# Rows of a second modulation: loaded two ahead of the low-rank factors, multiplied in the convolution's program order

## The chip, the cores and the metric

The kernel runs on one core of one Trainium2 chip. The metric is the time of one launch on the device, in microseconds (us). The engines are PE (TensorE, the matrix engine), DVE (VectorE), ACT (ScalarE), POOL (GpSimd) and SP (SyncE, which here only issues DMAs). Every engine works through its own instructions in order, and an instruction that waits holds back all that stand behind it on that engine.

## The reference

```python
x = L0_attn_u                                       # (4, 1024, 2048)
mod = (silu(L0_c) @ L0_wmod).reshape(4, 6, 1, -1)   # wmod: (2048, 6 * 2048)
sa, ca, ga, sb, cb, gb = (mod[:, i] for i in range(6))
ga, gb = ((2 * (g >= 0) - 1) * max(abs(g), 0.25) for g in (ga, gb))
h = layernorm(x) * (1 + ca) + sa
x = x + ga * (causal_conv(h, K) + D * h)            # K: S4 kernel of length 2048, along the last axis
h = layernorm(x) * (1 + cb) + sb
x = x + gb * (h @ W.T + bias + sum_e w[e] * (h @ A[e].T) @ Bf[e].T)   # w = coeffs * scales
```

So there are two modulated layers: a long convolution along the 2048 features, and a 2048 x 2048 linear layer with 16 low-rank updates. The first layer needs sections 0, 1 and 2 of `mod`, the second needs sections 3, 4 and 5.

## The kernel before

The 4096 rows of x are taken as 32 tiles r of 128 rows.

**Modulation.** Section by section (1, then 0 and 2, later 4, 3 and 5), `wmod` is read as 16 rows of 128 x 2048 float32 (1 MB each) per section. `mod_load` (L320) issues such a row on SP's DMA queue, and `mod_mm` (L325) multiplies it: four matmuls of 32 output rows, side by side in the array, which add into one PSUM tile `modps`. The rows of the second modulation take turns in the `WM = 3` buffers of the pool `wmp`, so a fourth load waits on SP until the first product has been made.

**Convolution.** For each tile r: load (`conv_load`, L563), statistics (L548 to L72), normalisation (L558), then `conv_prep`: PE transposes in four quarters (L579), ACT applies scale and shift (L583) and casts to float16 (L593), DVE makes the remainders (L594) and the sums (L591). `conv_mm` then multiplies (L616) with Toeplitz blocks of K in three families, into PSUM tiles `ya` and `yb`; ACT copies the first family out as `qs` (L629), DVE finishes y (L633 to L643). `conv_post` stores y to DRAM (L658) and lets ACT take its squares (L662). x of tile r+2 is loaded while tile r is multiplied. Tiles 0 and 1 are multiplied early, with the first modulation's products between them, and are finished late (L652, L653).

**Low-rank merge.** `prep_lora` loads A (`la`, 2 MB, SP queue, L434) and squares it on ACT (L440), then loads B (`lb`, 2 MB, ACT's own queue, L449), scales it on ACT (L453), squares it (L457), scales again (L467) and casts (L468). `merge` (eight times) adds the product of the factors (PE `lps`, L494) to a block of W (loaded by L486) and writes seven Strassen blocks to DRAM.

**Linear layer.** From about 930 us on, a Strassen multiplication (L752) reads these blocks.

**Order.** A scheduler builds the order of each engine: it takes instructions by their place in the program (their priority) and by when its own cost estimates say that they can start. `tc.issue_after(i)` keeps what is inside it behind instruction `i` in that order; it adds no wait of its own on the chip. Inside tile r, `PLAN` tells at ten ticks what is to be issued beside the multiplication. "S" calls `step()`, which on every second call from tile 3 on advances `rest()`: two steps of the merge, then one row of `section(sec, (wmp,))` (load and product together), and so on:

```python
if r > EARLY and calls[0] % 2 == 0:
    with tc.issue_after(k.lasta.ins), tc.issue_after(k.lastv.ins):
        next(fill)
```

Here `lasta` and `lastv` are the last copy of `qs` and the last L633 of the convolution so far.

Of the kernel before, what the change touches and what calls it, by code (L numbers as in the profile page):

```python
# [34 lines left out]
class Net:  # L35
# [561 lines left out]
    def conv_mm(self, pl, hs, x, tick, early, pace, y=None):  # L597
        nc, v = self.nc, self.nc.vector
        hc, hs = hs
        if y is None:  # L600
            y = pl["y"].tile([P, D], F32, tag="y", name="y")
        yv = y.rearrange("p (j e t) -> p j e t", e=2, t=P)
        if not early:
            gv = self.gat.rearrange("p (j e t) -> p j e t", e=2, t=P)
        sums = pl["sm"].tile([P, 2], F32, tag="sums", name="sums")

        def family(ps, f, q, first):
            pf = ps.rearrange("p j t -> p (j t)")
            last = 4 * q + 3
            for i in range(last + 1):  # L610
                o = P * max(0, i - 4 * q)
                k0 = P * max(0, 4 * q - i)
                with pace(3 * (512 - o)):
                    for x, z in ((0, 0), (0, 1), (1, 0)):
                        h = hs[x][:, i] if f == 0 else hc[x][:, 2 * i + 2 - f]
                        nc.tensor.matmul(  # L616
                            pf[:, o:512], h, self.kf[f][z][:, ds(k0, 512 - o)],
                            start=first, stop=(i == last and (x, z) == (1, 0)), skip_group_check=True,
                        )
                        first = False  # L620
                if i == 3 and q == 1:
                    tick()

        for q in range(2):
            jj = slice(4 * q, 4 * q + 4)
            pa = self.cps.tile([P, 4, P], F32, tag="pa", name="ya")
            family(pa, 0, q, True)
            qs = pl["t"].tile([P, 4, P], F32, tag="qs", name="qs")
            self.lasta = nc.scalar.copy(qs, pa)  # L629
            tick()  # L630
            pb = self.cps.tile([P, 4, P], F32, tag="pb", name="yb")
            family(pb, 2, q, True)
            self.lastv = v.tensor_tensor(yv[:, jj, 1, :], pb, qs, ADD)  # L633
            if not early:
                v.tensor_tensor(yv[:, jj, 1, :], yv[:, jj, 1, :], gv[:, jj, 1, :], MUL)
            tick()
            family(pa, 1, q, False)
            sl = ds(1024 * q, 1024)
            if early:
                nc.scalar.copy(yv[:, jj, 0, :], pa)  # L640
            else:
                v.tensor_tensor(yv[:, jj, 0, :], pa, gv[:, jj, 0, :], MUL)  # L642
                v.scalar_tensor_tensor(y[:, sl], y[:, sl], 1.0, x[:, sl], MUL, ADD, accum_out=sums[:, q : q + 1])  # L643
            tick()
        return y, sums
# [182 lines left out]
WM, WMS = 3, 3  # L828
# [17 lines left out]
def net(ctx: ExitStack, tc: tile.TileContext, io):  # L846
    nc = tc.nc
    k = Net(ctx, tc, io)
# [6 lines left out]
    def pool(stack, name, bufs, side="left"):  # L855
        return stack.enter_context(tc.tile_pool(name=name, bufs=bufs, side=side, reuse_waits="tile"))
# [6 lines left out]
    wmp = pool(right, "wm", WM, "right")  # L863
# [2 lines left out]
    k.kpool = pool(left, "kt", 1)  # L866
    k.prep_mod(msm)

    def section(sec, pools):
        for q in range(16):  # L870
            if q == 0:
                k.mod_begin()
            k.mod_mm(k.mod_load(pools[q % len(pools)], sec, q), q)
            yield
        if sec == 0:
            k.sa = k.mod_column(msm, k.kpool, "sa", 0.0)
            k.hinv = k.fold_scale(msm, k.ca, k.sa, "fs1")
        elif sec == 1:
            k.ca = k.mod_column(msm, k.kpool, "ca", 1.0)
        elif sec == 2:  # L880
            k.gas, (k.gad,) = k.mod_gate(msm, "gad")
        elif sec == 4:
            k.cb = k.mod_column(msm, k.cst, "cb", 1.0)
        elif sec == 3:
            k.sb = k.mod_column(msm, k.cst, "sb", 0.0)
        else:
            _, k.gbd = k.mod_gate(msm, "gbd", io["bias"])
        yield

    def merges():  # L890
        yield from k.prep_lora(pl["lora"], pl["mrg"])
        for c in range(HC):
            yield from k.merge(pl["lora"], pl["mrg"], c)
# [3 lines left out]
    def take(g, n):  # L897
        for _ in range(n):
            next(g, None)
# [13 lines left out]
    def prep(r, shift=True):  # L913
        return k.conv_prep(pl, r, xs[r], sts.pop(r), hs, shift)
# [15 lines left out]
    for _ in section(1, (wms, wmp)):  # L930
        if n in KT:
            with tc.issue_after(k.last.ins), tc.high_priority():
                take(toe, 1)
        if n == X0:
            load(0)
        n += 1
    with tc.high_priority():
        stats(0)
        k.early_scale(msm)
    load(1)  # L940
    rows = (x for sec in (0, 2) for x in section(sec, (wms, wmp)))
    p = prep(0, False)
    take(p, 1)
# [49 lines left out]
    y2 = stp.tile([P, D], F32, tag="kb", name="y2")  # L993

    def rest():
        mods = (x for sec in (4, 3, 5) for x in section(sec, (wmp,)))
        n = 0
        for _ in mer:
            yield
            n += 1  # L1000
            if n % MR == 0:
                next(mods, None)
                yield
        for _ in mods:
            yield
        k.ginv = k.fold_scale(msm, k.cb, k.sb, "fs2", k.winv)
        yield

    fill = rest()
    p2l = ExitStack()  # L1010
    pr, wc, lf = {}, {}, {}
# [44 lines left out]
    stats(3)  # L1056
    nxt = prep(3)
    take(nxt, 1)
    cols[0] = 0

    def behind(n):
# [143 lines left out]
```

## Time and profile before

| | |
|---|---|
| median of 3 runs | 2148.39 us (2144.52, 2148.39, 2148.89) |
| profiled execution | 2145.24 us, of which the span from first to last instruction is 2143.4 us |
| mean granted TensorE clock | 0.989 |
| busy, share of the span | PE 2075.1 us (97%), DVE 1307.7 us (61%), ACT 925.1 us (43%) |
| HBM | 329 MB read, 155 MB written, 226 GB/s over the span |
| products of all 96 modulation rows (L325) | 116.2 us of PE, 26.8 us of idle time before them |

A timeline row gives start and length in us, the engine, the line, the operation, output and inputs, how many instructions are merged in it, and in brackets how long the engine was idle before it and what ended that. A row of the windows view gives a stretch, its length, the busy time and count of PE, PE's weight loads, DVE, ACT and POOL, the granted clock (1.00 is full), the share of DMA time and GB/s.

### The profile page before, as it was taken

Reading aid. Unit: us, or ns where it says so; the run is one execution under the profiler, and the core shown is the slowest. Engines: PE = TensorE matmul, PEld = TensorE weight load, DVE = VectorE, ACT = ScalarE, POOL = GpSimd, SP = SyncE. Lnnn points to the kernel's source line nnn. Section 1 sums busy time; section 2 is a strip of 40 time slices with the busy share of each in tenths; the row PEclk is TensorE's granted clock in tenths of the full one; section 3 lists DMA queues with packets and bytes.
Section 4 is the critical chain, followed back from the end, with each engine's and each line's share of the span. In section 5 each row is a group of like instructions: output and inputs, shape, how many; then the busy total and the mean of one; then the engine's idle time right before and its main releaser. Section 6 shows DMA issues by size and latency. Waiting matters only on the chain.

```text
span 2143.4 us, 28478 instructions
## 1 busy us (share of the span) xinstructions
PE 2075.1 (97%) x11121; PEld 1021.8 (48%) x11121; DVE 1307.7 (61%) x2358; ACT 925.1 (43%) x1703; POOL 7.0 (0%) x19
## 2 busy tenths in 40 slices
PE   6998799999999999999999999999999999999999
PEld 1344354555445555644545545545444444444444
DVE  5529699998889999756565565565432323232323
ACT  1425786677756877655554454455200000000000
POOL 0000000000000000000000000000000000000000
PEclk8999999999999999999999999999999999999999
DMA  9995846786776554387465565564795545555542
GB/s 400 417 371 197 314 163 250 285 309 240 281 274 247 187 191 174 124 336 281 172 246 191 184 241 184 197 241 180 270 350 165 188 150 171 168 165 166 177 153 74
DMA packets 127812, 486.21 MB, mean 227 GB/s; under 512 B 13672, under 2 KB 14088, under 8 KB 96446
## 3 DMA queue, kind: packets, MB, share of 16 engines
q1 hardware_dynamic: 126624, 479.65, 61.4%
q10 hardware_dynamic: 526, 2.63, 0.3%
q8 instruction: 87, 1.43, 0.3%
q0 software_dynamic: 528, 2.11, 0.2%
q14 instruction: 47, 0.39, 0.0%
HBM read 329.04 MB, written 155.30 MB: 226 GB/s over the span
## 4 chain that ended last, share of the span: by engine, by line
PE 64%; DVE 13%; ACT 5%; DMA 4%; issue 2%; ACTq 0%; SPq 0%; DVEq 0%
PE fZ L752 22%; PE fX L752 15%; PE fY L752 15%; PE ya L616 4%; PE tp L702 3%; DVE wch L522 2%; PE lps L494 2%; PE yb L616 2%; ACT t L583 1%; DVE st L548 1%; DVE hc L594 1%; DVE y L643 1%; DMA x<-in_x 1%; DMA we<-in_WT 1%; DVE hs L594 1%
## 5 line engine op out<-in xcount | busy, mean ns | idle before, releaser
L752 PEld LDWEIGHTS <-lf 128*128 128x128 f16 x5400 | 528.4, 98 | 621.1 <-issue 3.3
L752 PE MATMUL fZ<-w,lf 128*128 128x512 f16 (+1 forms) x2328 | 513.8, 377 | 1.3 <-ACT p L760 0.8
L752 PE MATMUL fX<-w,lf 128*128 128x512 f16 x1536 | 342.8, 379 | 1.4 <-DVE y L642 1.4
L752 PE MATMUL fY<-w,lf 128*128 128x512 f16 x1536 | 342.0, 379 | 0.0
L616 PEld LDWEIGHTS <-hc 128*128 128x128 f16 x2304 | 214.0, 98 | 213.8 <-issue 51.3
L770 DVE TENSOR_TENSOR xo<-xo,gb 128x512 f32<-128x512 f32 x128 | 87.7, 690 | 237.7 <-DMA xo<-x1d 224.4
L583 ACT ACTIVATE t<-tp,sa,ca 128x128 f32<-128x128 f32 x480 | 189.3, 476 | 38.2 <-PE tp L579 31.7
L616 PE MATMUL ya<-kh,hs 128*128 128x512 f16 (+3 forms) x768 | 194.6, 327 | 6.0 <-ACT hs L593 4.1
L616 PE MATMUL ya<-kh,hc 128*128 128x512 f16 (+3 forms) x768 | 192.4, 328 | 7.0 <-ACT qs L629 6.7
L616 PE MATMUL yb<-kh,hc 128*128 128x512 f16 (+3 forms) x768 | 194.0, 328 | 0.3 <-DVE hc L594 0.3
L760 ACT COPY p<-fZ 128x512 f32<-128x512 f32 x64 | 37.2, 582 | 286.0 <-PE fZ L752 272.1
L616 PEld LDWEIGHTS <-hs 128*128 128x128 f16 x1152 | 106.8, 98 | 106.4 <-issue 20.6
L760 ACT COPY p<-fX 128x512 f32<-128x512 f32 x32 | 18.8, 586 | 317.2 <-PE fX L752 242.1
L704 ACT ACTIVATE gt<-tp,sb,cb 128x256 f32<-128x256 f32 x256 | 125.0, 576 | 62.0 <-PE tp L702 60.5
L325 PE MATMUL modps<-wm,sct 128*32 128x512 f32 x768 | 116.2, 646 | 26.8 <-DMA wm<-in_wmod 19.5
L616 PE MATMUL ya<-kl,hc 128*128 128x512 f16 (+3 forms) x384 | 125.8, 328 | 0.0
L616 PE MATMUL yb<-kl,hc 128*128 128x512 f16 (+3 forms) x384 | 125.5, 327 | 0.0
L616 PE MATMUL ya<-kl,hs 128*128 128x512 f16 (+3 forms) x384 | 125.2, 326 | 0.0
L775 DVE TENSOR_TENSOR fin<-fX,gb 128x512 f32<-128x512 f32 x32 | 22.1, 692 | 127.4 <-PE fX L752 127.3
L594 DVE TENSOR_TENSOR hc<-t,hc 128x512 f16<-128x512 f32 x128 | 87.5, 684 | 8.2 <-ACT hc L593 7.9
L494 PE MATMUL lps<-lbh,lac 128*128 128x512 f16 x256 | 84.7, 379 | 5.4 <-DVE we L496 3.9
L715 DVE TENSOR_TENSOR lf<-gt,lf 128x1024 f16<-128x1024 f32 x64 | 76.7, 1219 | 18.1 <-ACT lf L714 18.1
(274 smaller groups left out, 2224.7 us busy)
## 6 DMA issues: line engine op xcount, KB each, us to landing
wm<-in_wmod SPq DMA_DIRECT2D x96, 1024.0 KB
lfd<-lf SPq DMA_DIRECT2D x112, 512.0 KB
lf<-lfd SPq DMA_DIRECT2D x112, 512.0 KB
x<-in_x SPq DMA_DIRECT2D x32, 1024.0 KB
x1d<-y SPq DMA_DIRECT2D x32, 1024.0 KB
x<-x1d SPq DMA_DIRECT2D x32, 1024.0 KB
xo<-x1d SPq DMA_DIRECT2D x128, 256.0 KB
out<-xo SPq DMA_DIRECT2D x127, 256.0 KB
```

The costliest lines, as they stand in the source:

```text
L325: self.last = self.nc.tensor.matmul(self.modps[32 * g : 32 * g + 32, :], self.sct[:, j].rearrange("p r b -> p (r b)"), w[:, ds(512 * g, 512)],
L494: nc.tensor.matmul(ps, la[:, x, k, h], y[:, k, osl], start=(n == 0), stop=(n == 5))
L522: v.tensor_tensor(hl[:, :, 1, :], tv, hl[:, :, 0, :], SUB)
L583: nc.scalar.activation(t[:, k], tp[:, k], AF.Identity, bias=self.sa[:, c, b : b + 1], scale=self.ca[:, c, b : b + 1],)
L594: v.tensor_tensor(lo[:, sl], src, hi[:, sl], SUB)
L616: nc.tensor.matmul(pf[:, o:512], h, self.kf[f][z][:, ds(k0, 512 - o)], start=first, stop=(i == last and (x, z) == (1, 0)), skip_group_chec ...
L702: nc.tensor.transpose(tp[:, c, r], xs[r][:, ds(P * (c0 + c), P)], self.ident)
L704: nc.scalar.activation(t[:, c0 + c], tp[:, c], AF.Identity, bias=self.sb[:, c0 + c, b : b + 1], scale=self.cb[:, c0 + c, b : b + 1],)
L715: v.tensor_tensor(hl[:, :, 1, :], s, hl[:, :, 0, :], SUB)
L752: nc.tensor.matmul(ps[name][:, cols], lf[i][:, k, x, :], wc[i][k // 4][:, k % 4, y, cols], start=(first and n == 0), stop=(n == 3 * HC - 1 ...
L760: nc.scalar.copy(t, ps[name])
L770: v.tensor_tensor(x, x, self.gbias[:, h], ADD)
```

## The change

The rows of sections 4, 3 and 5 are taken from one list, `order`. `fetch()` issues the load of the next row of that list and puts it into `ahead`. Ahead of the loop over tiles, two rows are fetched, behind the last load issued before (`k.lastw`). Each step of a section then makes the product of the oldest fetched row, kept behind the last matmul of the convolution that has been written so far (`lastc`), and fetches one more row. Sections 1, 0 and 2 work as before. `self.lastc` is new in `conv_mm`.

```diff
-                        nc.tensor.matmul(
+                        self.lastc = nc.tensor.matmul(
...
-    def section(sec, pools):
+    def section(sec, pools=None):
         for q in range(16):
             if q == 0:
                 k.mod_begin()
-            k.mod_mm(k.mod_load(pools[q % len(pools)], sec, q), q)
+            if pools:
+                k.mod_mm(k.mod_load(pools[q % len(pools)], sec, q), q)
+            else:
+                with tc.issue_after(k.lastc.ins):
+                    k.mod_mm(ahead.pop(0), q)
+                fetch()
             yield
...
+    order, ahead = [(sec, q) for sec in (4, 3, 5) for q in range(16)], []
+
+    def fetch():
+        if order:
+            ahead.append(k.mod_load(wmp, *order.pop(0)))
...
-        mods = (x for sec in (4, 3, 5) for x in section(sec, (wmp,)))
+        mods = (x for sec in (4, 3, 5) for x in section(sec))
...
     stats(3)
     nxt = prep(3)
     take(nxt, 1)
+    with tc.issue_after(k.lastw.ins):
+        for _ in range(WM - 1):
+            fetch()
```

## Prediction

> **What bounds the kernel now.** I read the busy times first: PE is busy for 2075.1 of 2143.4 us, so only 68 us can be won by removing waits, and PE work that leaves an idle stretch for a full one is paid in full. Then the windows view, cut where the changed products lie:
>
> ```profile
> 150.00:222.80 72.80, 62.32 (x373) 31.60 (x370) 59.57 (x132) 36.07 (x79) 0.56 (x1) 0.98 0.68 249
> 222.80:248.20 25.40, 15.10 (x92) 4.20 (x91) 8.50 (x23) 15.29 (x31) 0.00 (x0) 0.87 0.88 360
> 248.20:345.00 96.80, 93.18 (x549) 51.27 (x549) 90.26 (x188) 74.32 (x149) 0.61 (x1) 1.00 0.58 219
> 345.00:930.00 585.00, 570.02 (x3531) 309.04 (x3530) 520.54 (x1084) 413.97 (x850) 0.41 (x1) 1.00 0.63 233
> ```
>
> PE has 10.3 us free in 222.8 to 248.2, but only 3.6 in the 96.8 us after. What fills and what ends the holes is in PE's timeline:
>
> ```profile
> 178.79 2.78 PE L325 MATMUL modps<-wm,sct 128*32 128x512 f32 x24
> 185.65 0.28 PE L616 MATMUL ya<-kh,hs 128*128 128x256 f16 x1 [4.08 <-ACT hs L593]
> ...
> 222.79 3.11 PE L325 MATMUL modps<-wm,sct 128*32 128x512 f32 x22
> 225.83 0.66 PE L579 MATMUL tp<-ident,n 128*128 128x128 f32 x4
> 233.55 1.91 PE L325 MATMUL modps<-wm,sct 128*32 128x512 f32 x2 [7.07 <-DMA wm<-in_wmod]
> 239.34 0.39 PE L616 MATMUL ya<-kh,hs 128*128 128x512 f16 x1
> 248.21 0.38 PE L616 MATMUL ya<-kh,hc 128*128 128x512 f16 x1 [0.66 <-ACT qs L629]
> ```
>
> The 7.07 us look like the cost of a late weight row. But ACT's and DVE's timelines of the same stretch show another chain:
>
> ```profile
> 221.07 0.41 ACTq L449 DMA_DIRECT2D lb<-in_BfT  x1
> 233.41 3.89 ACT L453 ACTIVATE lb<-lb,lwt 128x2048 f32<-128x2048 f32 x2 [9.86 <-DMA lb<-in_BfT]
> 238.25 0.39 ACT L593 CAST hs<-sm 128x256 f16<-128x256 f32 x1
> 247.57 0.59 ACT L629 COPY qs<-ya 128x512 f32<-128x512 f32 x1
> ```
> ```profile
> 238.66 0.42 DVE L594 TENSOR_TENSOR hs<-sm,hs 128x256 f16<-128x256 f32 x1 [11.76 <-ACT hs L593]
> ```
>
> ACT waits for the low-rank factor B; the casts of tile 5 stand behind that wait; DVE waits 11.76 us for them; PE's `ya` at 239.34 needs their result. From 233.41 to 248 ACT is without a gap of half a microsecond, and its `qs` releases PE at 248.21. I call 248.21 the mark. So the products sit in a hole that ACT makes.
>
> **Which products move.** In the order of instructions before, 12 of the 48 rows of the second modulation are multiplied ahead of the mark, 36 behind it. In the changed order two are ahead of it and 46 behind; the last product keeps its place, near the end of the convolution. Ten rows move from the hole into the full stretch. Nothing else is added to PE.
>
> **Cost of a moved row.** At 349.84 a convolution matmul starts (this kind repeats every 0.215 us), the product starts at 350.15, and the next convolution matmul at 351.15. Without the product it would start at 350.06, so a row costs 1.09 us. Ten rows: +10.9 us, say +11.0.
>
> **What the old place saves.** Ahead of the mark nothing, unless ACT gets there sooner. The three products at 178.79 lie before a wait for ACT that ends at 185.65 either way (PE then idles 6.9 instead of 4.1 us). Those at 185.97 (1.92 us, a single matmul that stood apart) and 202.28 (1.07 us) shorten PE's way to 212.00, but there it waits 1.19 us for DVE, which is itself held until 210.46 by the small loads of `lws`, issued at the same place as before. One product still stands there. From 222.79 on PE would idle longer: saved 0.
>
> A longer hole may cool PE: at 186 to 188 the windows show a clock of 0.50 after the 4.08 us idle, at 188 to 190 0.66. So about 3.4 us run near half rate; the matmuls slowed are again ahead of the 212.00 wait, so I put 0 here, and 1.7 us (half of 3.4) only if that cover is gone.
>
> The Trainium skill (TensorE: Matmul & The Clock Gate, "Why this matters for your kernels") says to avoid idle gaps over about 3 us between bursts, because one idle window returns the array to half clock. It speaks against taking filler products out of these holes. By it the longer hole would cost one more cold window of about 3.4 us, an estimate of 1.7 us; the sum would be 9.2 instead of 7.5.
>
> **Where the mark goes.** It follows the landing of `lb`, which took 12.34 us from its issue at 221.07. In that time the DMA engines moved about 420 GB/s x 12.34 us = 5.2 MB, of which 2.1 were `lb` and 3.1 SP's. After the change fewer rows are in the way: SP's order has the same three rows first, then the 4th and 5th, each waiting for a product, where before nine 1 MB rows went out from 217.70 to 247.9. I count for the changed kernel at 221: some 0.7 MB left of the 5th row, x of tile 7 (1.0 MB) and two pieces of A (0.5 MB), 2.2 MB. 4.3 MB at the same rate are 10.2 us, 2.1 us sooner. One cast of tile 5 (0.63 us, before at 222.92) now stands behind `lb` on ACT: +0.6. Mark: -1.5 us.
>
> Bounds of this term: with `lb` alone on the engines 2.1 MB / 0.42 = 5.0 us plus some 2.3 of fixed time (from issue to first effect, by the 2.35 us wait on small loads), 5 us sooner. The order also puts ACT's squares of A ahead of the squares of tile 3; should A be there by 209, when ACT ran dry, `lb` could be issued at 217.5 (after tile 3's squares, whose input is ready at 215.1), 3.5 us sooner. Together -8.5 + 0.6 = -7.9. On the other side the 4th row, which can now go out right behind A, may hold A back; with 1 MB at 420 GB/s that is +2.4. I take -1.5, near the value with unchanged issue, since A was at 200 GB/s on the way from 202 to about 214.
>
> **What the idle time behind the mark takes up.** 3.6 us are free between 248.2 and 345, of which 1.41 wait for ACT's `qs` and 1.59 for DVE's n. DVE is 93% busy there, so a slower PE makes these shorter: between 0 and -3.6; I take -2.0. Behind 345 a product per two merge steps runs as before.
>
> **Moved past, and new waits.** The SP queue: a load waits for the product three rows before it, and holds what is behind. Products are now later, so the 4th load stands behind A and ahead of the store of tile 3; its condition (first product, near 199 us) is met before. The third piece of A for the merges is issued earlier and waits for DVE's L483 (252.5 before); behind it are row 6, the store of tile 4 (data ready at 257), x of tile 8 (buffer free at 259.5) and W's first block (buffer free near 265). Their own conditions come later: 0. The tiny loads of `bias` move ahead by some places: 0. On POOL nothing is moved. Every product from row 4 on has its data some 10 us before, so no product waits for DMA.
>
> **Sum.** +11.0 - 2.0 - 1.5 = +7.5 us, so the profiled 2145.24 us become 2152.7. The mean of the three runs (2147.3) is 2.0 above the profiled execution; I forecast 2155. What the measurement can tell from no change is about 0.2%, 4.3 us.
>
> **Rivals.**
> *Faster: PE's wait for weights is the cause, not ACT.* For it: the waits view puts 9.2 us on the DMA of `wm`, and transposes stand behind products on PE. Between 222.79 and 248.21 PE has 25.4 us, less 10.2 of waits, less 10.1 of products: 5.1 us of other work. The mark would move from 248.2 to 227.9: 11.0 - 2.0 - 20.3 = -11.3, 2136 us. It decides from a mark 13.3 us earlier on. Against it: L593 at 238.25 sits behind L453 on ACT, and L453 waits for `lb`, which no product feeds. Chance 0.10.
>
> *No change to measure: the channel is freed.* `lb` lands 5 to 8 us earlier: 11.0 - 2.0 - (5 to 7.9) = +4.0 to +1.1, 2148 to 2151. For it: 3 to 6 MB of rows leave the queue. Chance 0.23.
>
> *Slower still: SP's queue.* A held piece of A makes row 6 or W's first block late, or A itself is held by the 4th row: +5 to +9 more, 2160 to 2164. For it: the wait at the third piece; against it: the later conditions listed above. Chance 0.15.
>
> *The change doesn't load sooner.* In both orders the first three rows have the same places on SP, directly behind the early loads of x; later rows are issued later than before. This is part of the forecast.
>
> The forecast itself has 0.52. The low end takes the mark at -7.9 and all 3.6 us taken up (-0.5: 2145), the high end SP's holding (2164); outside is mainly the first rival. Faster 0.10, same 0.23, slower 0.67.
>
> **What the changed profile would show.** PE: no L325 at 178.79; about 6.9 us idle until 185.65; a wait for ACT in place of the 7.07 for `wm`, none on `wm` at all. ACT: L453 still waits for `lb`, to about 231; PE's `ya` after `qs` near 246.7. Behind it, ten L325 rows before the place of today's 335.88, and PE at 99% there. Wrong if the mark is before 240, if the stretch to tile 10 is not about 9 us longer from the mark on, or if PE waits for DMA behind it.

## The result, and the profile after

The changed kernel took 2159.54 us (median of 4 runs, 2157.51 to 2161.04), the kernel before 2148.01 us (2144.52 to 2148.89): a ratio of 1.0056, with a 95% interval of 1.0039 to 1.0074. It is slower by some 11.5 us. Seven later runs of the same changed kernel gave 2155.51 us and a ratio of 1.0045 (1.0028 to 1.0062); the two intervals overlap. The profiled execution took 2159.32 us, with a span of 2157.4.

The windows of the changed kernel, cut as those of before (stretch, length, busy time and count of PE, weight loads, DVE, ACT and POOL, granted clock, DMA share, GB/s):

```profile
150.00:222.80 72.80, 58.08 (x327) 29.72 (x325) 56.89 (x117) 30.57 (x69) 0.56 (x1) 0.91 0.54 199
222.80:248.20 25.40, 12.48 (x63) 5.68 (x62) 9.72 (x32) 18.12 (x33) 0.00 (x0) 0.73 0.48 195
248.20:345.00 96.80, 92.23 (x554) 46.28 (x553) 85.07 (x180) 69.38 (x138) 0.60 (x1) 0.96 0.69 251
345.00:930.00 585.00, 570.30 (x3531) 308.76 (x3530) 518.89 (x1078) 412.09 (x854) 0.41 (x1) 1.00 0.63 233
```

In the first two stretches PE is busy 6.9 us less than before, DMA moves much less (195 instead of 360 GB/s in the second), and the clock is lower: 0.73 instead of 0.87 in the second, and 0.96 instead of 1.00 in the third, which nothing in the busy times would tell. In the last stretch PE is as busy as it was (570.30 and 570.02 us).

PE's timeline of the changed kernel shows what became of the holes. A row `x8` is one modulation row: its four matmuls count twice each.

```profile
189.80 0.39 PE L616 MATMUL ya<-kh,hs 128*128 128x256 f16 x1 [6.79 <-ACT hs L593]
...
203.86 1.06 PE L325 MATMUL modps<-wm,sct 128*32 128x512 f32 x8
...
215.12 1.06 PE L325 MATMUL modps<-wm,sct 128*32 128x512 f32 x8
...
241.37 0.61 PE L616 MATMUL yb<-kh,hc 128*128 128x512 f16 x1 [12.29 <-ACT hc L593]
246.70 0.28 PE L616 MATMUL yb<-kh,hc 128*128 128x256 f16 x1 [0.60 <-ACT hc L593]
250.83 0.58 PE L616 MATMUL ya<-kh,hc 128*128 128x512 f16 x1 [2.62 <-ACT qs L629]
257.81 1.06 PE L325 MATMUL modps<-wm,sct 128*32 128x512 f32 x8
```

Two rows are left ahead of the mark (the first `ya` after `qs`, now at 250.83). The wait for `wm` is gone, and a wait of 12.29 us for ACT stands in its place. Behind it ACT still waits for B, and DVE has a wait that before did not have; the lines are from the timelines of ACT and of DVE:

```profile
220.67 1.91 ACT L440 ACTIVATE la<-la 128x2048 f32<-128x2048 f32 x1 [7.32 <-DMA la<-in_A]
224.60 0.41 ACTq L449 DMA_DIRECT2D lb<-in_BfT  x1
235.87 3.90 ACT L453 ACTIVATE lb<-lb,lwt 128x2048 f32<-128x2048 f32 x2 [7.16 <-DMA lb<-in_BfT]
250.17 0.61 ACT L629 COPY qs<-ya 128x512 f32<-128x512 f32 x1
```
```profile
235.60 0.69 DVE L548 BATCH_NORM_STATS2 st<-x 128x6 f32<-128x512 f32 x1 [7.76 <-DMA x<-in_x]
```

**How to compare these times.** The first 178 us hold none of the products that moved, and yet differ between executions: PE's wait for `hs` of tile 3 ends at 185.65 us in the profile of before, at 189.80 after, and anywhere from 182.69 to 189.80 in all the kernels below. So I count from that point (the `ya` matmul at 185.65 before) to the mark, and from the mark to the end of the span. In all the kernels PE makes the same matmuls in each of the two stretches, but for the products of the modulation.

| kernel | wait for `hs` ends, us | from there to the mark | mark to end of span |
|---|---|---|---|
| before | 185.65 | 62.56 | 1895.2 |
| changed | 189.80 | 61.03 | 1906.6 |
| changed, second set (e8) | 186.68 | 63.88 | 1903.4 |
| change's loads only (e1) | 189.19 | 62.68 | 1894.6 |
| change's products only (e2) | 182.69 | 63.09 | 1907.1 |
| changed, ten rows doubled (e5) | 182.70 | 63.22 | 1914.2 |
| changed, ten rows narrow (e9) | 185.65 | 61.53 | 1895.6 |
| before, ten rows doubled (e6) | 186.01 | 67.32 | 1896.6 |
| before, ten rows narrow (e10) | 186.01 | 65.38 | 1896.3 |
| before, B used later (e3) | 188.59 | 58.15 | 1900.8 |
| changed, B used later (e4) | 183.46 | 56.19 | 1907.6 |
| e4 with three rows free (e7) | 189.02 | 44.41 | 1909.9 |

The loss of the change lies behind the mark: 8.2 to 11.9 us with the products in their new places (changed, e8, e2), nothing with them in the old ones (e1). The last column is good to some 2 us: behind the last matmul of the convolution every kernel has the same work, and that alone takes 1219.5 to 1222.0 us in these profiles.

### The profile page after: what moved, and what is told of

The parts are those of the page before. It is cut to its first block, busy times and chain, and to the rows that moved or that the text cites. A ratio compares the mean times of both kernels' runs of the same rounds, so it can differ in the third digit from the quotient of the medians.

```text
span 2157.4 us, 28474 instructions
## 1 busy us (share of the span) xinstructions
PE 2081.8 (96%) x11121; PEld 1024.2 (47%) x11121; DVE 1309.7 (61%) x2358; ACT 924.8 (43%) x1703; POOL 7.0 (0%) x19
## 4 chain that ended last, share of the span: by engine, by line
PE 69%; DVE 17%; DMA 6%; ACT 6%; issue 2%; SPq 0%; ACTq 0%; POOL 0%; DVEq 0%; POOLq 0%
PE fZ L752 23%; PE fX L752 15%; PE fY L752 15%; PE ya L616 5%; PE yb L616 3%; PE tp L702 3%; DVE wch L522 2%; PE modps L325 2%; DVE st L548 2%; DMA we<-in_WT 2%; ACT t L583 2%; DVE hc L594 1%; PE lps L494 1%; DVE y L643 1%; DMA x<-in_x 1%
## 5 line engine op out<-in xcount | busy, mean ns | idle before, releaser
L548 DVE BATCH_NORM_STATS2 st<-x 128x6 f32<-128x512 f32 x128 | 83.6, 680 | 12.4 <-DMA x<-in_x 12.4
```

The lines of the kernel that those rows point to most:

```text
L548: v.bn_stats(st[:, q], x[:, ds(512 * q, 512)])
```

## The experiments

My theory: the ten products that moved were free in the hole that ACT makes while it waits for `lb`, and cost their whole length in the full stretch; the loads cost nothing by themselves. The rivals: the loads (or SP's queue) are the cost; PE's wait for weights is the cause of the hole; the loss comes from something else than the length of the products. Each ratio below is against runs of the kernel before that belong to the same set of experiments; their medians are 2147.66 us (for e1 to e4), 2148.03 (e5 to e7) and 2147.09 (e8 to e10).

### The two parts apart

e1 takes the change's loads, with products free to be placed as before:

```diff
-                with tc.issue_after(k.lastc.ins):
-                    k.mod_mm(ahead.pop(0), q)
+                k.mod_mm(ahead.pop(0), q)
                 fetch()
```

> Only the loads go ahead; the products keep the places that they had before (order of PE as before: twelve rows ahead of the mark). Theory (ten products moved from a hole into the full stretch cost the time): no change, 2148 us, ratio 0.998 to 1.002, and the hole of 222 to 248 us with ACT's wait for lb is still there. Rival (the loads, by their new places on SP's queue, cost the time): about as slow as the changed kernel, 2155 to 2160.

2148.69 us, ratio 1.0001 (0.999 to 1.0013): no change. On SP's queue seven rows now go out one after the other from 221.49 us on, where before five did. These are not the places of the changed kernel, since a load still waits for the product three rows before it. Its PE timeline still has the filled hole, and ACT's the wait:

```profile
237.58 1.92 PE L325 MATMUL modps<-wm,sct 128*32 128x512 f32 x2 [5.83 <-DMA wm<-in_wmod]
```
```profile
237.44 3.89 ACT L453 ACTIVATE lb<-lb,lwt 128x2048 f32<-128x2048 f32 x2 [10.11 <-DMA lb<-in_BfT]
```

e2 is the kernel before, with load and product of a row issued together as there, but the product kept behind the convolution (`lastc` is kept as in the change):

```diff
-            k.mod_mm(k.mod_load(pools[q % len(pools)], sec, q), q)
+            w = k.mod_load(pools[q % len(pools)], sec, q)
+            with tc.issue_after(k.lastc.ins) if sec > 2 else nullcontext():
+                k.mod_mm(w, q)
```

> Only the products of the second modulation are kept behind the convolution's matmuls; each load stands beside its product as before. Theory: as slow as the changed kernel, 2157 to 2162 us (ratio 1.004 to 1.007), since PE's order is the changed kernel's. Rival (the loads cost the time): near 2148.

2160.09 us, ratio 1.0046 (1.0028 to 1.0064): the whole loss. PE's timeline of e2 has the long wait of the changed kernel:

```profile
236.33 0.61 PE L616 MATMUL yb<-kh,hc 128*128 128x512 f16 x1 [11.60 <-ACT hc L593]
```

The place of the products is the cost; with it held, moving the loads makes no difference that can be measured.

### The hole without the wait for B

Two extra steps of the merge between the load of B and its first use let ACT find B in place (e3 on the kernel before, e4 on the changed one):

```diff
         nc.scalar.dma_start(out=b, in_=io["BfT"].rearrange("(k p) o -> p k o", p=P))
         yield
+        yield
+        yield
```

> The kernel before, with the use of lb (L453) two steps of the merge later, so that it stands behind tile 5's casts on ACT. Theory (ACT's wait for lb makes the hole): tile 5's casts come some 10 us earlier and the hole shrinks; what then ends last is PE's own wait for wm until about 233.5, so the mark moves by -3 to -6 us: 2142 to 2145 us. Rival (PE's wait for wm alone makes the hole): no change, 2148.

> The changed kernel with the same later use of lb. Theory: no wait of PE for wm and no wait of ACT for lb; what ends last is DVE's wait for x of tile 7 (235.6 in the changed kernel), so the mark moves by -5 to -8 us and PE's array stays cold for less long: 2150 to 2155 us. Rival (the hole does not depend on lb): 2159.

e3: 2144.94 us, ratio 0.9983 (0.9967 to 0.9998), the best median here, and below the kernel before by hardly more than the interval. Its mark is 4.4 us earlier, as expected, but in the profile (2149.26 us, one of the slower of the twelve runs) 5.6 us are lost again behind it, where almost three of the rows now stand. e4: 2150.83 us, ratio 1.0013 (1.0001 to 1.0025), so by medians the changed kernel gets back most of its loss when ACT doesn't wait. Counted from the `hs` point it is less: 1963.7 us against 1967.6 and 1967.3 (e8) of the changed kernel and 1957.8 of the one before. What it gets back lies ahead of the mark, 4.8 us against the first profile of the changed kernel; behind the mark it takes 1907.6 us, as e2 does. In e4's timelines the scaling of B (L455 there) has no wait ahead of it, and PE waits 8.29 us instead of 12.29; DVE's wait for x of tile 7 is the one that is left (PE's line is the first matmul behind the mark):

```profile
239.65 0.38 PE L618 MATMUL ya<-kh,hc 128*128 128x512 f16 x1 [0.30 <-ACT qs L631]
```
```profile
240.29 3.92 ACT L455 ACTIVATE lb<-lb,lwt 128x2048 f32<-128x2048 f32 x2
```
```profile
231.36 0.70 DVE L550 BATCH_NORM_STATS2 st<-x 128x6 f32<-128x512 f32 x1 [7.88 <-DMA x<-in_x]
```

So ACT's wait for B ended last in the hole, and without it the hole ends 4 to 5 us sooner; the rest of it stays, held by the next wait. In e3, where ACT no longer waits, that is PE's wait of 7.21 us for a `wm` row, and behind the mark ACT waits for PE (5.27 us for `tp`). The faster rival's picture comes true only once the wait for B is out of the way.

### The ten rows doubled and cut

e5 and e6 add rows 2 to 11 of the section for cb twice, in the changed kernel and in the one before:

```diff
-    def mod_mm(self, w, j):
-        for g in range(4):
+    def mod_mm(self, w, j, n=1):
+        for g in [0, 1, 2, 3] * n:
...
-                    k.mod_mm(ahead.pop(0), q)
+                    k.mod_mm(ahead.pop(0), q, 2 if sec == 4 and 2 <= q < 12 else 1)
```

> Changed kernel in which rows 2 to 11 of the first section of the second modulation (cb) are added twice (so cb is another than the reference's): 40 more matmuls, the ten rows that the change moved, each at its new place in the full stretch behind 248 us. Theory (a product in the full stretch costs its whole length, 1.09 us, and slowed PE takes up hardly any idle time): 10.9 us above the changed kernel, about 2170, between 2168 and 2172. Rival (idle time behind the mark takes part of it up, as the prediction's term of -2.0 had it, and a second copy finds the array in a better state): at most 2167.

> Kernel before in which the same rows 2 to 11 of section cb are added twice: 40 more matmuls, ten rows at the old places, nearly all ahead of the mark at 248 us, in time that PE spends waiting for the scalar engine's casts. Theory (the old place is a hole that the wait for the low-rank factor B makes, so products there cost nothing): 0 to 3 us above the kernel before, 2148 to 2151; the mark stays within 1.5 us of where it was, measured from the end of the wait for hs of tile 3. Rival (a row costs 1.09 us wherever it stands, and the change lost its time elsewhere): +10.9, about 2159.

e5: 2162.93 us, 1.0062 (1.0049 to 1.0076): +3.4 us over the first four runs of the changed kernel, where the theory had +10.9. The theory's number is missed, and the rival's (at most 2167, with a cheaper second copy) is met. The second copy is cheaper than the first: PE's timeline of e5 has both copies of a row in 1.92 us, where one takes 1.06, so ten second copies are 8.6 us:

```profile
252.93 1.92 PE L325 MATMUL modps<-wm,sct 128*32 128x512 f32 x16
```

By the profiles, e5 against e2 (whose marks differ by 0.14 us) is 7.1 us longer from the mark on. The rest of the gap may lie in the runs of the changed kernel that it is compared with; e8 repeats them.

e6: 2152.14 us, 1.001 (0.9998 to 1.0023): +4.1 us by medians, where 0 to 3 was expected, though the interval still holds no change. Not entirely free: from the mark on it is as before (1896.6 against 1895.2), but the mark came 4.8 us later, since 8.6 us more fill the hole to its end (PE has no idle time from 244.63 to the mark at 253.33). So the hole takes about half of that load, and the expectation for the mark was missed. At the full price of a row it would have been +10.9 us.

e9 and e10 leave the ten rows in place and cut their products to 16 of 512 columns:

```diff
-                self.modps[32 * g : 32 * g + 32, :],
+                self.modps[32 * g : 32 * g + 32, :n],
...
-                w[:, ds(512 * g, 512)],
+                w[:, ds(512 * g, n)],
...
-                    k.mod_mm(ahead.pop(0), q)
+                    k.mod_mm(ahead.pop(0), q, 16 if sec == 4 and 2 <= q < 12 else 512)
```

In e10 the same argument is added to the call of the kernel before.

> The changed kernel once more, with more runs, since the doubled rows came out at only +3.4 us by medians but +7.1 us from the mark to the end in the profiles. If the first four runs of the changed kernel all had a late start (its profile reached tile 3's wait for hs at 189.80 us, others at 182.7 to 185.7), its median is 2154 to 2158 here, 6 to 9 us above the kernel before, and the doubled rows cost 5 to 9 us. If not, 2159 to 2161, and they cost 2 to 4.

> Changed kernel in which the products of rows 2 to 11 of section cb take 16 of 512 columns (the other columns of these rows are left out of cb). Loads, waits and the number of matmuls stay. Theory: the moved rows cost what they take in the full stretch: 9 to 11 us below the changed kernel, so within 2 us of the kernel before, 2146 to 2150. Rival (the change costs by something else than the length of these products, such as the clock behind the longer wait or the vector engine's wait for x): at most 5 us below the changed kernel.

> Kernel before with the same ten rows cut to 16 columns at the old places. Theory: time in the hole is free, so taking the work out of it saves 0 to 3 us: 2145 to 2148. Rival (rows cost their length wherever they are): 2137 to 2139.

e8, the changed kernel again: 2155.51 us (2150.16 to 2163.36). Its profile starts earlier than the first (186.68 against 189.80), and against its median e5's doubled rows cost 7.4 us, close to the 7.1 of the profiles.

e9: 2149.61 us, 1.0014 (1.0005 to 1.0023): 5.9 us below e8 by medians, 7.8 from the mark on. A narrow row still takes 0.26 us, so no more than 8.0 could go:

```profile
253.18 0.26 PE L325 MATMUL modps<-wm,sct 128*32 128x16 f32 x8
```

The time fits the theory's bounds; the difference to the changed kernel, 5.9 by medians and 7.8 by the profiles, lies between the rival's 5 and the theory's 9 to 11, which had not counted what a narrow row still takes. From the mark on, e9 is back at the time of before (within the 2 us that the column is good to), although its loads and its waits ahead of the mark are those of the change (13.36 us for ACT `hc`).

e10: 2149.40 us, 1.0014 (1.0002 to 1.0025). Taking the work out of the hole saved nothing, so the rival (2137 to 2139) is out; it even cost 2.3 us. With short products the buffers of `wmp` come free sooner, SP issued its next five rows in 14.64 us instead of 21.23, and B took 14.35 us from its issue to ACT's use of it, not 12.34. The mark was 2.8 us late. That the one caused the other fits the trace and wasn't tested further. The short products also leave the clock low: it is 0.50 from 228 us up to the mark, and the convolution's first matmuls behind the mark start every 0.43 us, twice the 0.215 of before:

```profile
251.39 0.59 PE L616 MATMUL ya<-kh,hc 128*128 128x512 f16 x1 [1.79 <-ACT qs L629]
251.77 0.63 PE L616 MATMUL ya<-kl,hc 128*128 128x512 f16 x1
252.20 1.06 PE L616 MATMUL ya<-kh,hc 128*128 128x512 f16 x2
```

The 17th of them is 1.5 us later behind the mark than before. Here no row has moved, so this is the price of the clock by itself; by the 400th 0.6 us of it are left, as PE is idle 0.8 us less.

### A version with three rows in the first hole

e7 is e4's kernel with two more steps between A's load and its squares, and the first three products free:

```diff
+        yield
+        yield
...
-                with tc.issue_after(k.lastc.ins):
+                with nullcontext() if sec == 4 and q < 3 else tc.issue_after(k.lastc.ins):
                     k.mod_mm(ahead.pop(0), q)
```

> Changed kernel with two more steps of the merge between the load of A and its squares, two more between the load of B and its use (as in the late-B runs), and the first three products of cb not kept behind the convolution, so that they go into the idle stretch of about 7 us ahead of tile 3's hs. Theory: the late-B version of the changed kernel (2150.8) less three rows of 1.09 us that leave the full stretch, and less part of the vector engine's wait for x of tile 7 (7.9 us there), since the squares of tile 3 stand ahead of those of A again and x can be loaded sooner: 2142 to 2148. Rival (the vector engine's wait was hidden and the three rows only push the hs of tile 3 back): 2149 to 2152.

2147.17 us, 0.9993 (0.9982 to 1.0003): in the theory's bounds, and not to be told from the kernel before. The three rows stand ahead of `hs` again, at 182.16. But the hole has moved: the mark comes 18 us sooner than before, and 14.7 us of this are lost again behind it. ACT does B's work there and is busy without a break from 248 to 261, and PE waits for `qs`:

```profile
182.16 2.78 PE L325 MATMUL modps<-wm,sct 128*32 128x512 f32 x24
260.74 0.59 PE L620 MATMUL ya<-kh,hc 128*128 128x512 f16 x1 [5.06 <-ACT qs L633]
```

## Why the prediction was right, point by point

**Ten rows into the full stretch, +10.9 us.** Right. e2 has the loss with the products alone, e1 has none with the loads alone. e9 takes 0.8 us per row out and is 7.8 us shorter from the mark on; e5 puts 0.86 us per row in and is 7.1 us longer than e2. Both are close to the length of what was taken or put, and the count below comes to 1.03 us a row, so the price per row holds.

**Nothing saved ahead of the mark.** Right. PE is idle 6.79 us at `hs` (6.9 forecast), and e10, with the ten rows almost gone from the old place, has no earlier mark. The place is free only for what fits: twice the rows (e6) move the mark by 4.8 us.

**Idle time behind the mark taken up, -2.0.** Right in size. In the 96.8 us from the mark on, PE had 3.6 us free before; after:

```profile
250.83:347.60 96.77, 94.82 (x571) 48.05 (x571) 85.32 (x178) 67.83 (x134) 0.60 (x1) 0.97 0.72 258
```

That is 1.95 us free, so -1.7; the same sum gives -2.0 in e8.

**The cold clock, 0.** This step failed. I looked at the first hole, whose slow matmuls lie ahead of another wait, and put 1.7 us only where that cover is gone. The second hole ends at the mark and has no cover. The windows of before from 242 to 254 (first fence) and of the changed kernel from 242 to 258 (second; last three columns: clock, DMA share, GB/s):

```profile
242.00:246.00 4.00, 2.38 (x20) 1.00 (x20) 2.47 (x7) 3.75 (x11) 0.00 (x0) 1.00 1.02 420
246.00:250.00 4.00, 2.86 (x18) 1.09 (x18) 3.37 (x10) 4.00 (x13) 0.61 (x1) 1.00 1.01 426
250.00:254.00 4.00, 4.00 (x29) 2.58 (x28) 4.00 (x10) 1.11 (x4) 0.00 (x0) 1.00 0.82 336
```
```profile
242.00:246.00 4.00, 4.00 (x11) 1.25 (x10) 0.80 (x4) 4.00 (x11) 0.00 (x0) 0.50 0.00 0
246.00:250.00 4.00, 1.58 (x13) 0.81 (x13) 2.73 (x6) 4.00 (x12) 0.00 (x0) 0.93 0.02 4
250.00:254.00 4.00, 3.17 (x8) 1.13 (x8) 3.72 (x10) 2.80 (x9) 0.60 (x1) 0.50 0.00 0
254.00:258.00 4.00, 4.00 (x21) 1.83 (x23) 1.99 (x7) 2.00 (x1) 0.00 (x0) 0.72 0.24 61
```

The clock of before also fell to 0.50 in the 7.07 us wait, but the products brought it back by 238 us and kept it at 1.00 up to the mark. Without them it stays at 0.50 from the 12.29 us wait until 246, recovers, and falls again behind the waits of 0.60 and 2.62 us before the mark. From 250.83 to 256.30 the convolution's matmuls start every 0.43 us instead of 0.215: half of 5.5 us, 2.7 us lost in the full stretch. In e8 the slow part behind the mark is shorter (clock 0.50 from about 252 to 255: 1.7 us). The Trainium skill (TensorE: Matmul & The Clock Gate, "Why this matters for your kernels") warns of idle gaps over about 3 us. That fits the first fall, in the 12.29 us wait; the second, which costs the time, comes behind shorter waits, the longest 2.62 us. The estimate that the prediction made with it, 1.7 us, is what e8 shows and 1 us less than the first trace, while my sum had 0. e10 shows 1.5 us of such a loss with no row moved. e4 has the clock at 1.00 behind the mark without the products, and yet is no shorter from there on (1907.6); but there ACT's work on B also lies behind the mark, so e4 doesn't give the price.

With it the sum is 10.9 - 1.7 + 2.7 = 11.9 us behind the mark, measured 11.4 (1906.6 - 1895.2), and for e8 10.9 - 2.0 + 1.7 = 10.6, measured 8.2. That the first comes so close is partly luck, as a count by work shows. Up to the 330th convolution matmul behind the mark PE has the same 438 entries in both kernels, and in the changed one 80 more, the ten rows (before, then changed):

```profile
248.21:324.18 75.97, 73.95 (x438) 41.31 (x438) 71.19 (x151) 60.47 (x118) 0.61 (x1) 1.00 0.50 188
```
```profile
250.83:338.77 87.94, 86.89 (x518) 43.14 (x518) 78.11 (x158) 61.73 (x119) 0.60 (x1) 0.97 0.69 246
```

| us, against before, up to the 330th matmul | changed | e8 | e2 |
|---|---|---|---|
| longer by | 11.97 | 10.62 | 11.26 |
| of this the clock (lag of the 17th matmul, ahead of any product) | 2.66 | 1.68 | 2.69 |
| idle time of PE | -0.97 | -1.35 | -1.71 |
| left for the ten rows | 10.28 | 10.29 | 10.28 |

So a row costs 1.03 us, in three executions alike. Up to the 400th matmul, near 345 us in the profile of before, 1.6 us of the loss come back in all three: 0.7 of idle time, and 1.0 because the kernel before multiplies one row there in two parts (at 335.88 and 337.93). That leaves +10.3, +9.0 and +9.6 us. What is added behind that, +1.0, -0.7 and +2.3 us up to the end, falls on the same work as before, and stays open; e1, with no row moved, has -0.6 there.

**The mark, -1.5.** The profile shows exactly that (61.03 against 62.56 us), but by luck, for it doesn't hold: e8 has +1.3, e2 +0.5, e5 +0.7, e9 -1.0. The count of bytes was right (4.3 MB forecast from issue to use; 372 GB/s x 11.27 us = 4.2 MB after, 330 x 12.79 = 4.2 MB in e8). The step that failed is the rate: I kept 420 GB/s, and the engines moved less when less was queued. So B's trip took 11.27 to 12.79 us, not 10.2, and the term is about 0. The "2.3 of fixed time" in its bounds was misread: 2.35 us is DVE's idle time, while the small loads that ended it at 210.46 had been issued from 199.14 on.

**No new wait.** On SP right: no product waits for DMA behind the first modulation, and the time from 345 on is as before within some 2 us. Missed: in the new order the squares of tile 3 stand behind those of A on ACT, x of tile 7 was issued 36.8 us after the `hs` point instead of 31.6, and DVE's statistics waited 7.76 us for it. In the changed kernel DVE then still waits 1.60 us for ACT's cast, so it was hidden; in e4 it is the longest wait ahead of the mark on DVE.

**The forecast time.** 2155 us against 2159.54 and 2155.51; the sum in the first profile is +11.4 - 1.5 = +9.9 us from the `hs` point on, forecast +7.5. The rest of the 14.0 us between the two profiled spans is the start, 4.15 us. The sum was too small by the clock, taken as 0, and by the mark, taken as -1.5; the price per row, the largest term, was right. That the second median falls on the forecast is luck: its seven runs lie between 2150 and 2163 us. The rivals: "PE's wait for weights" is out by e1 and e2 for these kernels (the mark moved by 1.5 us at most in them and in the changed kernel); "the channel is freed" is out since B came hardly sooner; "SP's queue" is out since in the changed kernel PE has no wait for DMA between 250 and 930 us, and since e9, with the change's loads, lost nothing from the mark on.

## What to carry to other kernels

Before filler work is moved off an idle stretch, ask who makes the stretch: if another engine does, the filler is free there as far as it fits, and is paid in full elsewhere, however its own wait reads. Then look at where the stretch ends. If it ends in front of full work, an emptier hole also costs the slow clock behind it. And where two executions differ ahead of the change, count from a common instruction, not from the start of the span.

## What the runs showed of the hardware

- The clock doesn't follow the length of the idle time alone. After the same 3.25 us wait the same four matmuls of L676 (`x8`) took 3.70 us before and in e2, 6.75 in the changed kernel and 5.25 in e7, ahead of the products that moved. This is a part of the spread at the start.
- Before, little work held the clock: PE was busy 2.38 and 2.86 of 4 us in two stretches with short waits, and the clock stayed at 1.00. With 1.58 of 4 us busy in the changed kernel it fell again to 0.50. About as much work did not bring it back in e10: PE was busy 2.34 of 4 us from 246 to 250, and the clock stayed at 0.50.
- Less traffic hardly brought a large load in sooner: B's 2 MB took 12.34 us to their use with 423 GB/s on the engines, and 12.79 us (e8) with 330; with 372 in the changed kernel's first profile it was 11.27.
- Repeating the same four float32 matmuls at once costs 0.86 us, where the first time costs 1.06.
